# A hybrid state-space and attention network on one core: the seed of the norms' inverse square root moved from VectorE to ScalarE

## The chip, the cores and the metric

The kernel runs on one core of a Trainium2 chip. A core has TensorE (matrix products, PE in the profile), VectorE (DVE), ScalarE (ACT), GpSimd (POOL) and SyncE (SP, which here only issues DMA transfers). The engines have queues of their own, each in program order, and wait for each other through semaphores. The metric is device time in microseconds of one execution; less is better.

## The reference, cut to what matters

The network has four layers on an input of 4 images, 96 channels, 64 x 64 pixels. The first is a state-space layer with two blocks, each of which begins with a norm over the 96 channels of every pixel:

```python
mu = seq.mean(-1, keepdims=True)
var = ((seq - mu) ** 2).mean(-1, keepdims=True)
h = (seq - mu) * jax.lax.rsqrt(var + EPS) * ln_g + ln_b
xz = h @ in_w
...
dA = jnp.exp(delta[..., None] * A)
dBx = delta[..., None] * Bm[:, :, None, :] * xc[..., None]
hstates = jax.lax.associative_scan(comb, (dA, dBx), axis=1)[1]
y = jnp.einsum('blds,bls->bld', hstates, Cm) + Dp * xc
```

The recurrence runs over the 4096 pixels of an image, for 192 channels with 16 states each. A sparse quadratic layer and two attention layers with feed-forward parts follow; the change does not touch them.

## The kernel before

`_mamba` computes the first layer, `_back` the rest; the state-space stage takes the first 3120 us or so of the span. In it the pixels are cut into 8 chunks of 512. A **unit** is one chunk of one pair of images in one of the two blocks: 32 units. A unit has 24 **steps** (three groups of channels, four rows, two halves): 768 steps. `steps` lists them, and one loop over them emits the instructions of all engines in an order written out by hand (`tc.manual_schedule()`), so that each engine's program order is fixed when the kernel is built.

What a step s does, by the names of the code:

- `copies`: SP brings the step's decays in a DMA of 512 KB with a broadcast (tile `a`, six buffers, L434), five steps ahead; now and then also `db`.
- `broadcasts`: TensorE spreads the step's inputs over the 128 partitions into PSUM (tile `pq`, three buffers, L447), two steps ahead. `pq` of step s+2 reuses the buffer of step s-1, so it waits for that step's scans.
- `decays`: ScalarE takes the exponential (L452).
- `product`: VectorE multiplies `pq` by the broadcast B (L457). In the steps that `apart` picks, four of a unit, GpSimd does it on `db` instead.
- `scans`: VectorE runs two scans of 512 (tile `hs`, L470), and between them the next step's product. GpSimd multiplies the states by C (tile `hc`, L476). `hs` and `hc` hold two steps each, in two buffers: a scan two groups later needs that `hc` has read the old `hs`.
- `states` (ScalarE, L480) keeps the last state, `reduce` (TensorE, `py`, L488, every second step) sums over the states, into four groups of 32 partitions, `gate` (VectorE L496, GpSimd L497, every eighth step) finishes y.

Beside the steps there is side work of the units to come: generators `norm`, `front`, `tail` and `rest`, of which the class `Side` advances one in a slot of each step. A generator hands its slot on with a `yield "gap"`. `front` makes the next unit's inputs; among its GpSimd work are `du` (L339) and `ul` (L355), each three per unit. `rest` puts two bn_stats (L408) on VectorE in the units of the first image pair or the second, every other unit or so.

`norm` makes the normalized input of the unit after next. TensorE subtracts the mean (`mm_xc`), ScalarE squares, TensorE forms the variances `mm_v` of 2 images x 512 pixels as a tile of 128 x 8, and ScalarE adds epsilon (`ve`, L221). Then the inverse square root is made by Newton's method from a guess that comes from the bits of the float: half of the bit pattern, taken from a constant. VectorE does that guess (L223, L224) and half of the negative variance (`vh`, L225); GpSimd does three Newton steps in twelve small instructions (L227 to L230). ScalarE copies three columns of history in the same slot (`hn`, L234). TensorE spreads the result over the channels (`mm_r`, L240), one image at a time since PSUM has one buffer for `mm`, and VectorE multiplies (`hn`, L249), once for each image.

Of the kernel before, what the change touches and what calls it, by code (L numbers as in the profile page):

```python
# [9 lines left out]
F32 = mybir.dt.float32  # L10
F32R = mybir.dt.float32r
I32 = mybir.dt.int32
# [3 lines left out]
AF = mybir.ActivationFunctionType  # L16
ALU = mybir.AluOpType
# [25 lines left out]
def _load(nc, pool, src, shape, name, dtype=F32):  # L43
    t = pool.tile(shape, dtype, name=name, tag=name)
    nc.sync.dma_start(t, src)
    return t


def _mamba(ctx, tc, io, w, fd, fstats, xsums):
# [9 lines left out]
    nc = tc.nc  # L59
    wp = ctx.enter_context(tc.tile_pool(name="mw", bufs=1))  # L60
# [30 lines left out]
    red = _load(nc, wp, io["k_red"].rearrange("c (j m) -> c j m", j=4), [128, 4, 32], "red")  # L91
    ctr = _load(nc, wp, io["k_center"], [C, C], "ctr")
    low = _load(nc, wp, io["k_low"], [128, 2], "low")
    mean1 = wp.tile([C, 1], F32, name="mean1", tag="mean1")
    nc.gpsimd.memset(mean1, 1.0 / C)

# [73 lines left out]
    def tag(unit):  # L170
        return "_".join(map(str, unit))

    def mm(nm, unit, shape=None):
        return ps_mm.tile(shape or [128, TC], F32, name=f"mm_{nm}{tag(unit)}", tag="mm")

    def tl(nm, unit, shape, dtype=F32, bufs=1, to=None):
        return work.tile(shape, dtype, name=f"{nm}_{tag(unit)}", tag=to or nm, bufs=bufs)
# [9 lines left out]
    def norm(unit):  # L187

        ch, l, pr = unit
        bs = (2 * pr, 2 * pr + 1)  # L190
        xc, sqs, ps = {}, {}, {}

        def centred(n):
            xc[n] = tl(f"xc{n}", unit, [C, TC])
            nc.scalar.copy(xc[n], ps[n])
            sqs[n] = tl(f"sq{n}", unit, [C, TC])
            nc.scalar.activation(sqs[n], xc[n], AF.Square)

        for n, b in enumerate(bs):
            ps[n] = mm(f"xc{n}", unit, [C, TC])  # L200
            nc.tensor.matmul(ps[n], ctr, seq[b, ch, l], start=True, stop=True)
            if l == 0:
                nc.scalar.activation(
                    tl("xs", unit, [C, TC], to=f"sq{n}"), seq[b, ch, 0], AF.Identity, accum_out=xsums[:, b, ch : ch + 1]
                )
            yield
            centred(n)
            yield "free" if n == 0 else "gap"
        p_v = mm("v", unit, [128, 8])
        for n in range(2):  # L210
            for j in range(4):
                nc.tensor.matmul(
                    p_v[:, n * 4 + j : n * 4 + j + 1], sqs[n][:, j * 128 : (j + 1) * 128], mean1, start=True, stop=True
                )
        yield
        ve = tl("ve", unit, [128, 8])
        it = tl("it", unit, [128, 8], I32)
        r = tl("r", unit, [128, 8])
        vh = tl("vh", unit, [128, 8])
        a = tl("ra", unit, [128, 8])  # L220
        nc.scalar.activation(ve, p_v, AF.Identity, bias=w["eps"])  # L221
        yield "gap"
        nc.vector.tensor_single_scalar(it, ve.bitcast(I32), 1, op=ALU.logical_shift_right)  # L223
        nc.vector.tensor_scalar(r.bitcast(I32), it, -1.0, float(0x5F3759DF), ALU.mult, ALU.add)  # L224
        nc.vector.tensor_scalar(vh, ve, -0.5, None, ALU.mult)  # L225
        for _ in range(3):
            nc.gpsimd.tensor_tensor(a, r, r, ALU.mult)  # L227
            nc.gpsimd.tensor_tensor(a, a, vh, ALU.mult)
            nc.gpsimd.tensor_scalar(a, a, 1.5, None, ALU.add)
            nc.gpsimd.tensor_tensor(r, r, a, ALU.mult)  # L230
        if ch:
            for b in bs:
                hn = hn_buf[b, l]
                nc.scalar.copy(hn[:, 0:3], hn[:, TC:])  # L234
        yield "gap"
        yield "gap"
        for n, b in enumerate(bs):
            p = mm(f"r{n}", unit, [C, TC])
            for j in range(4):
                nc.tensor.matmul(  # L240
                    p[:, j * 128 : (j + 1) * 128],
                    r[:, n * 4 + j : n * 4 + j + 1].to_broadcast([128, C]),
                    ident,
                    start=True,
                    stop=True,
                )
            yield
            yield
            nc.vector.tensor_tensor(hn_buf[b, l][:C, 3:], p, xc[n], ALU.mult)  # L249
            yield "free"  # L250
# [283 lines left out]
    with tc.manual_schedule():  # L534
        for n in (0, 1):
            load(units[n])
        side.front = [weights(0), norm(units[0]), front(units[0])]
        side.drain()
        for s in range(5):
# [7 lines left out]
        for s in range(n_steps + NS):  # L547
# [5 lines left out]
            if at == 0:  # L553
                if n + 1 < len(units) and n + 1 not in late:
                    side.front += ([norm(units[n + 1])] if n == 0 else []) + [front(units[n + 1])]
                    side.norm += [weights(1)] * (n == 0)
            if at == 22 and n + 1 == len(units):
                side.tail.append(way_out(units[n]))
            if at == 3 and 0 < n < len(units):
                if n + 1 in late:  # L560
                    side.front = [tail(units[n - 1]), norm(units[n + 1]), front(units[n + 1])]
                else:
                    side.tail.append(tail(units[n - 1]))
# [5 lines left out]
            if s + 2 < n_steps:  # L569
                unit, k, r, h = steps[s + 2]  # L570
# [16 lines left out]
            if live and s + 5 < n_steps:  # L587
                unit, k, r, h = steps[s + 5]
# [807 lines left out]
@with_exitstack  # L1396
def kernel(ctx: ExitStack, tc: tile.TileContext, io, out):
    nc = tc.nc
    cp = ctx.enter_context(tc.tile_pool(name="common", bufs=1))
    dp = ctx.enter_context(tc.tile_pool(name="scratch", bufs=1, space=DRAM))  # L1400
    w = _shared(nc, cp, io)
    p2 = [[dp.tile([2 * C, TC], F32, name=f"p2_{b}_{n}", tag=f"p2_{b}_{n}") for n in range(NCH)] for b in range(B)]
    fd = [dp.tile([C, L], F32, name=f"fd_{b}", tag=f"fd_{b}") for b in range(B)]
    with tc.tile_pool(name="stats", bufs=1) as fp:
        fstats = fp.tile([C, B, NCH, 6], F32, name="fstats", tag="fstats")
        xsums = fp.tile([C, B, NCH], F32, name="xsums", tag="xsums")
        with ExitStack() as c:
            _mamba(c, tc, io, w, fd, fstats, xsums)
        with ExitStack() as c:
            _back(c, tc, io, w, fd, fstats, xsums, p2, out)  # L1410
# [143 lines left out]
```

## Time and profile before

| | us |
|---|---|
| median of 3 runs | 5290.37 (5288.55 to 5313.22) |
| profiled execution | 5277.23 |
| its span, first to last instruction | 5275.4 |
| busy: VectorE | 4432.0 (84% of the span) |
| busy: TensorE | 4055.2 (77%) |
| busy: GpSimd | 2988.1 (57%) |
| busy: ScalarE | 2695.1 (51%) |

The page divides the span into 40 slices of 132 us and gives the busy share of each in tenths. A row of the groups has the line of the code, the engine, the operation, out<-in with shapes, then the busy time, the mean of one instruction in ns, and the idle time of the engine just before, with what ended it. A row of a timeline has the start in us, the duration, the engine, the line, and in brackets the idle time before it and its releaser. "L470" is line 470 of the code of the kernel before.

### The profile page before, as it was taken

Reading aid. Unit: us, or ns where it says so; the run is one execution under the profiler, and the core shown is the slowest. Engines: PE = TensorE matmul, PEld = TensorE weight load, DVE = VectorE, ACT = ScalarE, POOL = GpSimd, SP = SyncE. Lnnn points to the kernel's source line nnn. Section 1 sums busy time; section 2 is a strip of 40 time slices with the busy share of each in tenths; the row PEclk is TensorE's granted clock in tenths of the full one; section 3 lists DMA queues with packets and bytes.
Section 4 is the critical chain, followed back from the end, with each engine's and each line's share of the span. In section 5 each row is a group of like instructions: output and inputs, shape, how many; then the busy total and the mean of one; then the engine's idle time right before and its main releaser. Section 6 shows DMA issues by size and latency. Waiting matters only on the chain.

```text
span 5275.4 us, 52716 instructions
## 1 busy us (share of the span) xinstructions
PE 4055.2 (77%) x15440; PEld 1763.8 (33%) x15440; DVE 4432.0 (84%) x5735; ACT 2695.1 (51%) x5085; POOL 2988.1 (57%) x2104
## 2 busy tenths in 40 slices
PE   4676767777777777777777636899898889989776
PEld 2122222222222222222222102345454555545565
DVE  2879999999999999999999777878787978787655
ACT  3465656656565565656656420023453545444566
POOL 2778888888888888888888761002130312112122
PEclk7677767677786777767777658999999999999976
DMA  4778878788888878788788674553324233322110
GB/s 99 171 171 197 198 187 203 194 196 201 197 192 195 200 190 194 189 195 202 184 201 202 148 192 139 171 170 100 99 85 145 90 102 94 98 90 76 57 33 21
DMA packets 314045, 800.18 MB, mean 152 GB/s; under 512 B 52247, under 2 KB 58106, under 8 KB 312702
## 3 DMA queue, kind: packets, MB, share of 16 engines
q1 hardware_dynamic: 310174, 790.53, 59.2%
q10 hardware_dynamic: 3584, 6.29, 0.4%
q8 instruction: 123, 2.02, 0.2%
q14 instruction: 164, 1.34, 0.1%
HBM read 703.83 MB, written 67.63 MB: 146 GB/s over the span
## 4 chain that ended last, share of the span: by engine, by line
PE 26%; DVE 26%; issue 17%; ACT 11%; POOL 8%; DMA 5%; SPq 1%; DVEq 0%; POOLq 0%; ACTq 0%
DVE hs L470 12%; PE py L895 10%; DVE pq L457 6%; ACT a L452 3%; DMA a<-ddl 3%; POOL hc L476 3%; PE mm_i L264 2%; DVE z L880 2%; DVE a L1110 2%; PE px L1177 2%; PE ph L1092 2%; PE pa L1078 2%; PE py L488 1%; POOL t L1248 1%; POOL o L1246 1%
## 5 line engine op out<-in xcount | busy, mean ns | idle before, releaser
L476 POOL TENSOR_TENSOR hc<-hs,bc 128x1024 f32<-128x1024 f32 x767 | 1804.8, 2360 | 365.8 <-DVE hs L470 350.0
L470 DVE TENSOR_TENSOR_SCAN hs<-a,hst,pq 128x512 f32<-128x512 f32 x1280 | 1571.9, 1261 | 28.9 <-ACT hst L480 12.8
L895 PE MATMUL py<-z,wk 128*96 128x512 f32 x2304 | 1113.5, 613 | 25.8 <-issue 14.3
L452 ACT ACTIVATE a<-a,aneg 128x512 f32<-128x512 f32 x1280 | 849.4, 712 | 309.5 <-DMA a<-ddl 307.4
L880 DVE TENSOR_TENSOR z<-cp,cp 128x512 f32<-128x512 f32 x1152 | 792.5, 714 | 183.9 <-PE py L895 169.3
L457 DVE TENSOR_TENSOR pq<-pq,bc 128x1024 f32<-128x1024 f32 x640 | 772.9, 1208 | 156.9 <-PE pq L447 156.9
L488 PE MATMUL py<-hc,red 128*32 128x512 f32 x3072 | 609.0, 865 | 14.3 <-POOL hc L476 14.3
L895 PEld LDWEIGHTS py<-z,wk 128*96 128x96 f32 x2304 | 366.5, 169 | 447.7 <-issue 315.6
L447 PE MATMUL pq<-uy,sel 64*128 64x512 f32 x768 | 253.4, 654 | 257.1 <-DVE hs L470 204.7
L1145 POOL MEMSET zz<- 96x2 f32 x16 | 1.6, 98 | 740.8 <-ACT zz L1154 739.4
L264 PE MATMUL mm_i<-hn,wk 97*128 97x512 f32 x512 | 348.7, 817 | 92.5 <-ACT xcv L275 59.7
L1246 POOL TENSOR_TENSOR o<-o,fb 128x384 f16<-128x384 f16 x64 | 70.1, 1096 | 549.4 <-ACT o L1251 549.4
L470 DVE TENSOR_TENSOR_SCAN hs<-pq,hst,db 128x512 f32<-128x512 f32 x256 | 324.8, 1269 | 58.1 <-issue 36.1
L452 ACT ACTIVATE pq<-a,aneg 128x512 f32<-128x512 f32 x256 | 177.1, 692 | 366.6 <-DVE hs L470 336.4
L457 POOL TENSOR_TENSOR db<-db,bc 128x1024 f32<-128x1024 f32 x128 | 301.8, 2358 | 21.8 <-DMA db<-ddu 20.3
L447 PE MATMUL pq<-ux,sel 64*128 64x512 f32 x512 | 166.4, 637 | 186.1 <-DVE hs L470 171.8
L447 PEld LDWEIGHTS pq<-uy,sel 64*128 64x128 f32 x768 | 93.8, 238 | 550.8 <-DVE hs L470 372.1
L264 PEld LDWEIGHTS mm_i<-hn,wk 97*128 97x128 f32 x512 | 117.2, 254 | 297.3 <-issue 204.2
L1177 PE MATMUL px<-bd,a 128*96 128x128 f32 x1024 | 148.6, 294 | 67.5 <-DVE a L1110 57.1
L1146 POOL TENSOR_TENSOR zz<-zz 96x256 f32<-96x256 f32 x128 | 122.3, 955 | 135.5 <-ACT zz L1153 83.4
L447 PEld LDWEIGHTS pq<-ux,sel 64*128 64x128 f32 x512 | 61.4, 232 | 384.7 <-DVE hs L470 275.4
L275 ACT ACTIVATE xcv<-mm_i,pvec 128x512 f32<-128x512 f32 x96 | 65.8, 685 | 213.8 <-PE mm_i L264 108.8
(286 smaller groups left out, 6645.8 us busy)
## 6 DMA issues: line engine op xcount, KB each, us to landing
a<-ddl SPq DMA_DIRECT2D x768, 512.0 KB, 7.3
cp<-p SPq DMA_DIRECT2D x480, 192.0 KB, 2.7
db<-ddu SPq DMA_DIRECT2D x128, 512.0 KB, 7.6
bc<-ddb SPq DMA_DIRECT2D x64, 512.0 KB, 8.4
cp<-p SPq DMA_DIRECT2D x480, 64.0 KB, 2.6
ddl<-dl SPq DMA_DIRECT2D x128, 192.0 KB, 3.5
tw_k_fwd<-in_k_fwd SPq DMA_DIRECT2D x64, 256.0 KB, 3.6
tw_k_inv<-in_k_inv SPq DMA_DIRECT2D x64, 256.0 KB, 3.0
```

The costliest lines, as they stand in the source:

```text
L264: nc.tensor.matmul(p, wt[:, 0:128], hn_buf[bs[k], l][:, cols], **f)
L447: nc.tensor.matmul(pqs[s][:, i, :], sel[rows, r, :], made[unit][6][k][h][rows], start=True, stop=True)
L452: nc.scalar.activation(to[:, i, :], das[s][:, i, :], AF.Exp, scale=acol(s, i))
L457: engine.tensor_tensor(t, t, bc(unit, 2, k, h), ALU.mult)
L470: nc.vector.tensor_tensor_scan(hss[g][:, at, :], d0[:, i, :], d1[:, i, :], hst[pr, l, g % 12][:, at : at + 1], ALU.mult, ALU.add)
L476: (nc.gpsimd if s + 1 < n_steps else nc.vector).tensor_tensor(hcs[g][:, sl, :], hss[g][:, sl, :], bc(unit, 3, k, h), ALU.mult)
L488: nc.tensor.matmul(pys[unit, k][32 * (i // 2 + i % 2 * 2) :][:32], red[:, r, :], hc[:, i, :], start=(r == 0), stop=(r == 3))
L880: nc.vector.tensor_tensor(zs[n], cps[q, r0], cps[q, r1], ALU.mult)
L895: nc.tensor.matmul(pys[q], wk[k // KG][:, k % KG, :], zs.pop(n), start=(k == 0), stop=(k == NE - 1))
L1146: nc.gpsimd.tensor_tensor(z0[:, :, 0, :], z0[:, :, 0, :], z1[:, :, 0, :], ALU.add)
L1177: nc.tensor.matmul(p[:, j, :], a2[i % 2][:, kk, :], tabs["bd"][:, int(kk > 0), :], start=True, stop=True)
L1246: nc.gpsimd.tensor_tensor(o2.rearrange("p j c -> p (j c)"), os.pop(g), d["fb2"], ALU.add)
```

## The change

The guess and the half of the negative variance are made on ScalarE. The bit pattern is read as an integer, multiplied by -0.5 and added to the constant, which comes as a bias from a new tile `magic`; the result is written as an integer. `vh` follows directly on `ve`; `r` comes after the generator's "gap", where VectorE's three instructions stood. The tile `it` falls away. GpSimd's Newton steps are the same, and now wait for ScalarE. In the new kernel's program ScalarE has 64 instructions more, VectorE 96 fewer, GpSimd one memset more; the order of all the others is the same on every engine, and the number of ScalarE's table loads too.

```diff
@@ _mamba
+    magic = wp.tile([128, 1], F32, name="magic", tag="magic")
+    nc.gpsimd.memset(magic, float(0x5F3759DF))
@@ norm
         ve = tl("ve", unit, [128, 8])
-        it = tl("it", unit, [128, 8], I32)
         r = tl("r", unit, [128, 8])
         vh = tl("vh", unit, [128, 8])
         a = tl("ra", unit, [128, 8])
         nc.scalar.activation(ve, p_v, AF.Identity, bias=w["eps"])
+        nc.scalar.activation(vh, ve, AF.Copy, scale=-0.5)
         yield "gap"
-        nc.vector.tensor_single_scalar(it, ve.bitcast(I32), 1, op=ALU.logical_shift_right)
-        nc.vector.tensor_scalar(r.bitcast(I32), it, -1.0, float(0x5F3759DF), ALU.mult, ALU.add)
-        nc.vector.tensor_scalar(vh, ve, -0.5, None, ALU.mult)
+        nc.scalar.activation(r.bitcast(I32), ve.bitcast(I32), AF.Identity, bias=magic, scale=-0.5)
         for _ in range(3):
             nc.gpsimd.tensor_tensor(a, r, r, ALU.mult)
```

## The prediction

> **What bounds the kernel now.** I read the page first (busy times and slices), then the groups by form in the state-space stage, then the timelines of VectorE, GpSimd and TensorE around one of the edited places.
>
> ```profile
> DVE  2879999999999999999999777878787978787655
> POOL 2778888888888888888888761002130312112122
> ```
>
> The change lies in the first 3120 us. There VectorE is busy nine tenths or more in most slices and GpSimd eight. The window from 395 to 2810 us, which holds 26 equal units of 92.9 us, gives VectorE 2271.9 of 2415 us (94%), GpSimd 2085.5 (86%), ScalarE 1467.9 (61%), the DMA engines 82%. So VectorE seems to set the pace, with GpSimd close behind.
>
> ```profile
> L224 DVE TENSOR_SCALAR r<-it 128x8 int32<-128x8 int32 x32 | 62.3, 1946 | 1.1
> L225 DVE TENSOR_SCALAR vh<-ve 128x8 f32<-128x8 f32 x32 | 33.8, 1056 | 0.0
> L223 DVE TENSOR_SCALAR it<-ve 128x8 int32<-128x8 int32 x32 | 24.8, 775 | 32.2 <-ACT ve L221 32.2
> ```
>
> These three are what the change takes away. Eight elements per partition should not take 1 to 2 us, and their shortest cases are 165, 172 and 159 ns. The medians are 903, 2275 and 1305 ns. The timeline of VectorE says where the rest goes:
>
> ```profile
> 1505.47 0.72 DVE L496 SCALAR_TENSOR_TENSOR y<-xcv,pvec,py 128x512 f32<-128x512 f32 x1
> 1506.11 0.91 DVE L223 TENSOR_SCALAR it<-ve 128x8 int32<-128x8 int32 x1
> 1507.05 2.27 DVE L224 TENSOR_SCALAR r<-it 128x8 int32<-128x8 int32 x1
> 1509.23 1.31 DVE L225 TENSOR_SCALAR vh<-ve 128x8 f32<-128x8 f32 x1
> 1510.46 1.27 DVE L470 TENSOR_TENSOR_SCAN hs<-a,hst,pq 128x512 f32<-128x512 f32 x1
> ```
>
> and that of GpSimd what it was doing meanwhile, and afterwards:
>
> ```profile
> 1504.47 2.51 POOL L339 TENSOR_TENSOR du<-dl,xcv 128x512 f32<-128x512 f32 x2
> 1506.94 2.35 POOL L476 TENSOR_TENSOR hc<-hs,bc 128x1024 f32<-128x1024 f32 x1
> 1509.25 1.27 POOL L497 TENSOR_TENSOR y<-y,zs 128x512 f32<-128x512 f32 x1
> 1510.47 1.27 POOL L339 TENSOR_TENSOR du<-dl,xcv 128x512 f32<-128x512 f32 x1
> 1511.70 0.20 POOL L227 TENSOR_TENSOR ra<-r 128x8 f32<-128x8 f32 x1
> ...
> 1515.06 2.35 POOL L476 TENSOR_TENSOR hc<-hs,bc 128x1024 f32<-128x1024 f32 x1
> 1517.37 1.28 POOL L355 TENSOR_TENSOR ul<-du,ux 128x512 fp32r<-128x512 f32 x1
> 1518.59 2.37 POOL L476 TENSOR_TENSOR hc<-hs,bc 128x1024 f32<-128x1024 f32 x1
> 1520.91 1.29 POOL L355 TENSOR_TENSOR ul<-du,ux 128x512 fp32r<-128x512 f32 x1
> 1522.13 4.86 POOL L476 TENSOR_TENSOR hc<-hs,bc 128x1024 f32<-128x1024 f32 x2
> ```
>
> The reader is to see two things. Each of the three ends as one GpSimd instruction ends (1506.94, 1509.25, 1510.47): VectorE stands still for 4.35 us. And GpSimd has no gap from 1502.15 to 1528.2: in just this part of the unit it is the fuller engine.
>
> [...] half of the four reductions takes as long as all four. The trace agrees: 1.93 us for x8 (at 1518.28), and where GpSimd came late:
>
> ```profile
> 3026.35 1.92 PE L488 MATMUL py<-hc,red 128*32 128x512 f32 x4 [4.05 <-POOL hc L476]
> ```
>
> **The change part by part.** *VectorE loses 96 instructions.* Start to next start, the three take 4.35 us in 23 of the 27 units from 394 to 2814 us, 3.20 to 4.26 in four: 115 us in all. In the five other units GpSimd is idle and they take 0.36 us.
>
> *How much of a unit's 4.35 us survives.* VectorE's order is otherwise the same in the built program, and so is GpSimd's. I replay the unit above with VectorE 4.35 us earlier. GpSimd's chain does not move: du, hc, y, du and the Newton steps (L227 to L230, 1511.70 to 1515.06) were never waiting for VectorE's three. The third hc after Newton still ends at 1524.5. Behind it, in TensorE's order, stand the reduction py (L488), then mm_r (L240) for the second image, and only then can VectorE do its second hn (L249), with the next scan queued behind. Earliest second hn = 1524.5 + 0.1 (semaphore) + py half (1.0 at the fast clock, 1.86 at the slow one; both occur) + mm_r to hn (2.06 wherever VectorE waited for it) = +3.2 to +4.0, I take +3.66. Today it starts at 1528.45, +3.95. So this unit keeps 0.3 us of 4.35; VectorE waits at hn instead. (A smaller stop on the way: the scan of the group after next needs hc's buffer read, 1517.4 against 1516.6.)
>
> Every second unit also has two bn_stats (L408) on VectorE there; in these the second hn starts +5.45 after the third hc on average, counted without GpSimd's own 0.19 us wait. They keep 1.8 us. Sum of the differences: 14 units without (mean 4.05) x 0.39 = 5.5, 13 with x 1.79 = 23.3: **29 us**. All at the slow clock (4.0) it is 20 us; with mm_r at the fast clock too (2.25) 67.
>
> *Starved units.* VectorE waits for ve in order in three units: 3.95 us at 111, 7.45 at 235, 15.36 at 2951. The scan behind it had its inputs (at 2951: exp done 2936.65, db 2935.03). Freed, VectorE does that step in the gap, and the broadcast pq on TensorE, which waited 3.9 us for it ahead of mm_r, no longer does. Newton's end (2955.39) then gates mm_r: first hn at 2957.4 instead of 2959.94, 2.5 us, and the same in the other two. **7 us**; at least 0 if these shifts meet a later wait, at most 15 (half of the 26.8 us waited, rounded up).
>
> *ScalarE gains 64 instructions.* Nearest row: ve, 267 ns, start to next start 0.17. No conversion from int32 on ScalarE is in the trace; a cast to fp32r of 512 columns takes 0.60 against 0.56 for a copy, so between 0.17 and 0.54 us each, I take 0.2. At most 35 us over a stage in which ScalarE idles 39%; the next exp waits 1.75 us for its DMA. Taken at nothing. No table load is added: 129 in both built orders.
>
> *The new wait:* Newton on GpSimd waits for r from ScalarE. In the built order r stands just before the copies hn (L234), which start at 1507.37, Newton at 1511.70; the smallest such margin in the 27 units is 3.5 us. Behind Newton on GpSimd stand the hc, and behind these VectorE's scans. Nothing, while the margin holds.
>
> *GpSimd gains one memset* (about 0.1 us, among the opening ones while loads are under way): nothing. The queue of SP issues the same; its copies a wait for VectorE's scans, 1242 us in all, and move earlier with these, except where they stand behind ux and uy, which wait for GpSimd's ul. With 82% of the DMA engines' time used, 40 us less in 3000 adds 1%: nothing.
>
> Sum: 29 + 7 = **36 us**. The profiled execution took 5277.2 us (span 5275.4 and 1.8 around it), 13 us under the median of the runs, 5290.4. Taken from the median: **5254 us**, 0.7% less. A measurement of this kernel can tell about 0.5%, 26 us, from no change.
>
> **The rivals.**
>
> *Full recovery.* VectorE's share of 94% says that it bounds, and 115 us come back, with the starved units' part about 125: 5165 us. For it: VectorE waits only 96 us for pq and 7 for mm_r from 395 to 2900 us. Against it: GpSimd's unbroken 26 us in each unit. Chance 0.12.
>
> *Nothing to measure.* TensorE stays at the slow clock behind the wait, units without bn_stats keep nothing, starved units give it back: 10 to 20 us, 5275. For it: most mm_r there took 2.06 us, the slow form. Chance 0.24.
>
> *Slower.* ScalarE reaches r late: the exp ahead of it waits for DMA a (12.3 us the longest, 285 in all). From 3.5 to 4.3 us of lateness on, each us delays Newton, hc, py and hn one to one, in the chain that now sets the pace. At 2 us beyond the margin in all 27 units it is +54: 5344. Against it: r's place was reached 3.5 us early in every unit. Chance 0.05.
>
> *It doesn't do what it says:* the built order shows it does; no chance given.
>
> The main case has 0.59.
>
> **How the numbers follow.** The main case runs from 20 + 0 to 67 + 15 us of gain: 5208 to 5270. The range 5185 to 5288 takes in most of the second rival and the lower part of a partial recovery, leaving out the full one and the slow one. Faster by over 0.5% (under 5264): 0.12 and 0.54 of the main case: 0.66. Within 0.5%: 0.24 and the other 0.05: 0.29. Slower: 0.05.
>
> **What would show it.** Right: L223 to L225 gone from VectorE, its busy time 121 us less, and of that most found again as waits of hn (L249) for mm_r, now 26 us, then about 110; GpSimd's hc waiting less than 329 us for scans; unit length about 91.8 us instead of 92.9. Wrong: if hn waits little and the unit shrinks to 88.6 us, VectorE was the bound after all; if GpSimd waits for r from ScalarE, the slow rival; if the three starved places keep their gap on VectorE, that step.

## The result, and the profile after

| | before | after |
|---|---|---|
| median of 12 runs each, us | 5287.37 | 5293.53 |
| ratio after / before, 95% interval | | 1.0013 [0.9996, 1.003] |
| profiled execution's span, us | 5275.4 | 5291.6 |
| VectorE busy, us | 4432.0 | 4322.7 |

The change makes no difference that can be measured. The forecast was 36 us less, and the interval excludes it: it reaches from 2 us less to 16 us more. VectorE was nevertheless relieved, by 109 us of busy time. The page of the kernel after, first VectorE's and GpSimd's slices, then the share of each engine in the chain that ended last:

```profile
DVE  2888898888988889888898877888787878787655
POOL 3778888888888888888898861002130322112122
...
PE 29%; DVE 19%; issue 14%; ACT 11%; POOL 10%; DMA 9%; SPq 2%; DVEq 0%; POOLq 0%; ACTq 0%
```

The share of each engine in the chain before the change:

```profile
PE 26%; DVE 26%; issue 17%; ACT 11%; POOL 8%; DMA 5%; SPq 1%; DVEq 0%; POOLq 0%; ACTq 0%
```

The row of nines of VectorE has become mostly eights; GpSimd's row is nearly what it was. In the chain VectorE fell from 26 to 19%, and DMA rose from 5 to 9%. From 395 to 2900 us alone, the DMA of `a` rose from 6.2 to 14.3% of the chain. The groups by form (busy time, mean ns of one, idle time before and what ended it) show the moved instructions and their neighbours:

```profile
L249 DVE TENSOR_TENSOR hn<-mm_r,xc 96x512 f32<-96x512 f32 x64 | 43.7, 683 | 76.4 <-PE mm_r L240 75.5
L227 POOL TENSOR_TENSOR ra<-r 128x8 f32<-128x8 f32 x96 | 19.3, 201 | 38.1 <-ACT r L225 15.9 <-ACT hst L480 11.7 <-ACT hn L234 5.5
L225 ACT ACTIVATE r<-ve,magic 128x8 int32<-128x8 int32 x32 | 9.5, 296 | 0.0
L223 ACT ACTIVATE vh<-ve 128x8 f32<-128x8 f32 x32 | 6.7, 209 | 1.0
```

So 16 us of busy time on ScalarE do what took VectorE 121. Of VectorE's three instructions before the change, each of the 79 cases that took over 0.4 us ended 0.03 us after the end of a GpSimd instruction; why is not shown. GpSimd's Newton steps waited for ScalarE in five units, 33.1 us in all (the row names `r` or a neighbour of it on ScalarE), in the same five in which they had waited 39.6 us for VectorE's `vh`. The wait of `hn` for `mm_r` grew from 26 to 76 us, where about 110 were forecast.

Where did the time go? The waits from 395 to 2900 us (engine and line, what it waited for: total us, times, longest) say it. ScalarE and VectorE after:

```profile
ACT a L452 <- DMA a<-ddl: 334.5, 183, 5.1
ACT pq L452 <- DMA a<-ddl: 231.4, 29, 9.4
...
DVE pq L457 <- PE pq L447: 171.6, 80, 4.7
DVE hn L249 <- PE mm_r L240: 44.0, 40, 2.4
```

and both before, in the same window:

```profile
ACT pq L452 <- DVE hs L470: 292.5, 81, 7.4
ACT a L452 <- DMA a<-ddl: 228.6, 144, 3.6
...
DVE pq L457 <- PE pq L447: 96.0, 66, 4.4
DVE hn L249 <- PE mm_r L240: 7.1, 14, 0.7
```

Before, the largest wait of the exponentials was for VectorE's scans, and that for the decays `a` came second, 229 us. After, they wait for the DMA of `a` in both forms, 566 us. VectorE's product waits 172 us for `pq` where it waited 96. The wait of SP for GpSimd's `ul`, which stands ahead of some of these DMAs in SP's queue, grew too. Before, then after:

```profile
SPq L345 <- POOL ul L355: 161.7, 54, 4.6
```

```profile
SPq L345 <- POOL ul L355: 249.4, 54, 8.4
```

The chain of waits of the kernel after, in order of time (start, us, what), passes through this place:

```profile
1448.17 5.62 DMA a<-ddl
...
1454.45 0.71 ACT a L452
1455.15 0.58 ACT xcv L275
1455.78 3.78 PE mm_i L264 x4
...
1526.85 1.24 POOL ul L355
...
1528.10 0.57 SPq L345
...
1531.99 7.79 DMA a<-ddl
```

It runs from GpSimd's `ul` to SP's copies of ux and uy, to the `a` behind them, 7.79 us on its way, and from an `a` over the exponential to the copy `xcv` that stands behind it on ScalarE, to TensorE's `mm_i`. VectorE's `hn`, the place at which the forecast let the saved time end, is not on it.

The same unit as in the prediction, in SP's timelines (the DMA issues). Before, VectorE's second `hn` starts at 1528.45:

```profile
1528.24 0.52 SPq L345 DMA_DIRECT2D ux<-ul  x1
...
1531.76 1.21 SPq L434 DMA_DIRECT2D a<-ddl  x2
```

and after:

```profile
1537.48 0.52 SPq L345 DMA_DIRECT2D ux<-ul  x1
...
1541.03 1.21 SPq L434 DMA_DIRECT2D a<-ddl  x2
```

VectorE's timeline after has the second `hn` of this unit, with the wait for `mm_r` ahead of it in brackets:

```profile
1536.12 0.69 DVE L249 TENSOR_TENSOR hn<-mm_r,xc 96x512 f32<-96x512 f32 x1 [1.23 <-PE mm_r L240]
```

`hn` comes earlier within GpSimd's work, but ux, uy and the `a` behind them do not: the pair of `a` starts 3.3 us after `hn` before and 4.9 us after it now. In the mean of the 23 units of the table below, the first `a` behind these copies is issued 2.7 us after `hn` before and 5.3 us now.

Cutting each unit at four events gives the balance. The table holds means over the units 5 to 27, in us, taken from the starts in the traces (even and odd units averaged apart, then together; one profiled execution of each kernel). The events are the second `hn`, ScalarE's first and second copy `xcv` (L275), the last instruction of Newton on GpSimd, and the next unit's second `hn`. The lower rows belong to the experiments. A unit's length is set by a few discrete waits, so a mean of one execution is uncertain by up to some 0.5 us in the sum, and 0.3 in the second and third stretch (estimated from the scatter of the units).

| kernel | hn to 1st xcv | to 2nd xcv | to Newton's last | to next hn | sum |
|---|---|---|---|---|---|
| before | 10.81 | 8.16 | 59.81 | 14.39 | 93.2 |
| after | 12.17 | 9.25 | 60.64 | 12.02 | 94.1 |
| a_stall | 11.03 | 8.20 | 59.85 | 14.15 | 93.2 |
| a_noseed | 12.15 | 9.15 | 60.68 | 12.07 | 94.0 |
| a_copies_first | 10.74 | 8.91 | 60.84 | 12.75 | 93.2 |
| a_deep7 | 10.74 | 9.16 | 60.52 | 11.78 | 92.2 |
| b_deep7 | 10.72 | 8.21 | 59.76 | 14.14 | 92.8 |
| a_reduce_later | 13.78 | 8.88 | 60.52 | 10.48 | 93.7 |
| a_deep7_reduce_later | 11.56 | 8.95 | 61.13 | 10.49 | 92.1 |
| a_newton1 | 11.57 | 8.58 | 57.76 | 12.75 | 90.7 |
| b_newton1 | 10.73 | 7.75 | 57.21 | 16.60 | 92.3 |
| a_deep7_newton1 | 10.74 | 8.74 | 58.24 | 12.79 | 90.5 |
| b_deep7_newton1 | 10.73 | 8.11 | 57.42 | 16.49 | 92.7 |

From before to after the last stretch shrinks by 2.4 us: this is what was saved. The first three grow by 1.4, 1.1 and 0.8: this is where it went. The difference of 0.9 us for each of the 23 units, 20 us, is about the 16 us by which the profiled span is longer; over many runs only some 6 us of it are left.

### The profile page after: what moved, and what is told of

Its sections match the earlier page's. It is cut to its first block, busy times and chain, and to the rows that moved or that the text cites. A ratio compares the mean times of both kernels' runs of the same rounds, so it can differ in the third digit from the quotient of the medians.

```text
span 5291.6 us, 52686 instructions
## 1 busy us (share of the span) xinstructions
PE 4093.0 (77%) x15440; PEld 1748.6 (33%) x15440; DVE 4322.7 (82%) x5639; ACT 2706.8 (51%) x5149; POOL 2990.1 (57%) x2105
## 3 DMA queue, kind: packets, MB, share of 16 engines
q8 instruction: 123, 2.02, 0.2%
## 4 chain that ended last, share of the span: by engine, by line
PE 29%; DVE 19%; issue 14%; ACT 11%; POOL 10%; DMA 9%; SPq 2%; DVEq 0%; POOLq 0%; ACTq 0%
PE py L895 10%; DVE hs L470 8%; DMA a<-ddl 7%; POOL hc L476 4%; DVE pq L457 4%; PE mm_i L264 3%; ACT a L452 3%; DVE z L880 2%; PE py L488 2%; PE px L1177 2%; DVE a L1110 2%; PE mm_i L267 2%; PE ph L1092 2%; PE pa L1078 2%; POOL du L339 1%
## 5 line engine op out<-in xcount | busy, mean ns | idle before, releaser
L488 PE MATMUL py<-hc,red 128*32 128x512 f32 x3072 | 671.2, 841 | 50.4 <-POOL hc L476 50.1
L264 PE MATMUL mm_i<-hn,wk 97*128 97x512 f32 x512 | 325.1, 768 | 152.5 <-ACT xcv L275 127.4
L275 ACT ACTIVATE xcv<-mm_i,pvec 128x512 f32<-128x512 f32 x96 | 65.5, 682 | 214.6 <-PE mm_i L264 123.4
L1177 PEld LDWEIGHTS px<-bd,a 128*96 128x96 f32 x1024 | 130.7, 176 | 113.2 <-DVE a L1110 70.4
```

Source lines behind the costliest of these rows:

```text
L264: nc.tensor.matmul(p, wt[:, 0:128], hn_buf[bs[k], l][:, cols], **f)
L488: nc.tensor.matmul(pys[unit, k][32 * (i // 2 + i % 2 * 2) :][:32], red[:, r, :], hc[:, i, :], start=(r == 0), stop=(r == 3))
L1177: nc.tensor.matmul(p[:, j, :], a2[i % 2][:, kk, :], tabs["bd"][:, int(kk > 0), :], start=True, stop=True)
```

## The experiments

The expectations speak of **theory A**: VectorE's stop was not what set the pace, because beside it there ran a chain of nearly the same length, GpSimd's unbroken work and, behind it, the copies of `a` that come late (called A1; A2 is a variant that blames TensorE's order, in which the reduction `py` stands ahead of the side work). The rivals are the cost of ScalarE's new instructions, and, where an expectation says so, other bounds. Ratios are to the kernel before on the same chip. Its own medians there lie between 5280 and 5288 us, so a difference in us between two experiments can be off by several us.

### One Newton step, with and without the change

```diff
-        for _ in range(3):
+        for _ in range(1):
```

a_newton1 makes this edit in the changed kernel, b_newton1 in the kernel before.

> The changed kernel with one Newton step on GpSimd instead of three (two of the three refinements of the inverse square root are left out, 8 of 12 small instructions, 2.25 us of GpSimd's time per unit). Theory A, GpSimd's unbroken stretch (du, hc, y, Newton, hc, ul) and what hangs on it in SP's queue set the pace of a unit: 29 units x 2.25 us, about 60 us less than the changed kernel's 5293, so 5235. Theory B, the pace is set by ScalarE, to which the change gave 0.5 us per unit: no difference, 5290. Theory C, VectorE is still the bound: no difference either.

> The kernel before with one Newton step instead of three (the same part is left out). Theory A says that before the change VectorE with its 4.35 us of standing still and GpSimd's stretch ran side by side and were about equally long; then a shorter stretch alone gives less than in the changed kernel: 0 to 25 us, 5262 to 5287. If the two kernels gain the same 60 us, GpSimd's stretch alone bounded before the change, too, and VectorE's three instructions never mattered.

Measured: a_newton1 5221.4 us, ratio 0.9856 [0.982, 0.9893], 72 us under the changed kernel. b_newton1 5253.7, 0.9934 [0.9903, 0.9964], 34 us under the kernel before, more than the 0 to 25 that were expected. Shortening GpSimd's work by about 2.3 us pays in both, twice as much where VectorE has no stop. The table shows why: in b_newton1 Newton ends 2.6 us earlier and the next `hn` takes 2.2 us longer from there (16.60 for 14.39). VectorE's own queue, with the stop in it, then sets `hn`. So before, it seems, two chains of nearly equal length met at `hn`.

a_newton1 shows the late `a` too. In its even units the first `xcv` comes 12.2 us after `hn` and a unit takes 93.9 us; in its odd units, 10.9 and 87.4. (Even and odd units differ in other work too: before, they took 94.5 and 91.8 us.)

### VectorE's stop put back, its result unused

```diff
+        it, r2, vh2 = tl("it", unit, [128, 8], I32), tl("r2", unit, [128, 8]), tl("vh2", unit, [128, 8])
+        nc.vector.tensor_single_scalar(it, ve.bitcast(I32), 1, op=ALU.logical_shift_right)
+        nc.vector.tensor_scalar(r2.bitcast(I32), it, -1.0, float(0x5F3759DF), ALU.mult, ALU.add)
+        nc.vector.tensor_scalar(vh2, ve, -0.5, None, ALU.mult)
         nc.scalar.activation(r.bitcast(I32), ve.bitcast(I32), AF.Identity, bias=magic, scale=-0.5)
```

> The changed kernel with VectorE's three instructions put back where they stood, now on tiles that nobody reads; the seed still comes from ScalarE. VectorE has its old order and stands still 4.35 us per unit again; ScalarE's 64 instructions and GpSimd's new wait remain. Theory A, the stop was hidden beside GpSimd's stretch and what follows it: as the changed kernel, 5285 to 5300. Theory B, the change did win on VectorE and lost as much on ScalarE: 30 us or more above the changed kernel, 5320 to 5400, since now both costs are paid.

Measured: 5282.7 us, ratio 1.0005 [0.9989, 1.0021]: the same as the kernel before and as the changed one. Its groups by form have VectorE's stop back:

```profile
L228 DVE TENSOR_SCALAR r<-it 128x8 int32<-128x8 int32 x32 | 62.4, 1949 | 1.1
```

and its ScalarE waits as it did before, not as after:

```profile
ACT pq L456 <- DVE hs L474: 284.6, 81, 7.4
ACT a L456 <- DMA a<-ddl: 225.7, 152, 3.6
```

The stop alone switches between the two pictures, row for row in the table (11.03 and 14.15 against 12.17 and 12.02), and the time stays. So in this kernel, with all else as it is, 105 us of busy time more or less on VectorE are free, and the late `a` is a result of their absence and not of ScalarE's new instructions, which a_stall keeps.

### No seed at all

a_noseed leaves out the guess on both engines; Newton starts from 1, with three steps of the same instructions. `magic` now holds minus half of epsilon.

```diff
-        nc.scalar.activation(ve, p_v, AF.Identity, bias=w["eps"])
-        nc.scalar.activation(vh, ve, AF.Copy, scale=-0.5)
+        nc.scalar.activation(ve, p_v, AF.Identity, bias=magic, scale=-0.5)
         yield "gap"
-        nc.scalar.activation(r.bitcast(I32), ve.bitcast(I32), AF.Identity, bias=magic, scale=-0.5)
...
+            seed = r if n else one
```

> The changed kernel with no seed at all: Newton starts from the constant 1 (left out: the guess from the bits, so that the inverse square root is less exact), and ScalarE makes minus half of the variance directly in its one old instruction. Neither VectorE's three nor ScalarE's two are in it. Theory A: as the changed kernel less at most ScalarE's 0.5 us in 29 units, 5278 to 5293. Theory B, ScalarE's two instructions took the gain: the 36 us of the prediction or more come back, under 5257.

Measured: 5301.5 us, ratio 1.0038 [1.0021, 1.0055], a little above what was expected and not below the changed kernel. Its picture is that of after:

```profile
ACT a L452 <- DMA a<-ddl: 351.7, 195, 4.7
ACT pq L452 <- DMA a<-ddl: 231.2, 28, 9.5
```

With ScalarE's 64 instructions gone, `a` is as late and the unit as long (94.0 us). They took nothing away.

### TensorE's order

a_reduce_later emits the reduction after the slot of side work, so that `mm_r` need not stand behind it; a_deep7_reduce_later does so with the seventh buffer of the next section.

```diff
-            if s % 2 == 1 and 2 < s <= n_steps + 1:
-                reduce(s // 2 - 1)
             side.slot()
             if n == 0 or n + 1 in late:
                 side.slot()
+            if s % 2 == 1 and 2 < s <= n_steps + 1:
+                reduce(s // 2 - 1)
```

> The changed kernel with reduce (py) emitted behind the slot of its step, so that on TensorE mm_r no longer stands behind a py that waits for GpSimd's hc. Nothing is left out. Theory A2, the wait of hn for mm_r takes the gain: that wait falls from 44 us to under 15, time 5250 to 5265. Theory A1, SP's queue and the a behind it set the pace: the wait at hn falls but the time found goes to the wait for pq, 5280 to 5300.

> The changed kernel with the seventh buffer for a and reduce behind the slot. Nothing is left out. If the late a and the wait at hn are the two things that took the gain, both together give more than the buffer's 43 us: 5205 to 5230. If side work on TensorE and ScalarE (mm_i, xcv, the two table loads, mm_o) is a third chain of the same length, no more than the buffer alone: 5240 to 5255.

Measured: 5309.1 us, ratio 1.0054 [1.0036, 1.0073], slower than the kernel before and than the changed one; with the buffer 5252.8, 0.9934 [0.9911, 0.9956], no better than the buffer alone. The wait of `hn` nearly goes, from 44 to 2.8 us from 395 to 2900 us, and others take its place: VectorE's `y` waits 79 us for the reduction, and GpSimd's `hc` waits for it to free its buffer:

```profile
POOL hc L476 <- PE py L488: 240.7, 87, 5.6
```

The wait for `pq`, to which A1 gave the time, did not grow (148 us after 172). Since the edit brings waits of its own, the two times alone do not refute A2, and the second of them is also what a third chain on TensorE and ScalarE would give. The table says more. In a_reduce_later `hn` comes 1.5 us sooner after Newton's end than in the changed kernel (10.48 for 12.02), but the first `xcv` does not: from Newton's end to it there are 24.3 us in one and 24.2 in the other. So `hn` is not what sets the `xcv` there; a wait that vanishes is no gain where it was not the last to end.

### A seventh buffer for `a`

a_deep7 (the changed kernel) and b_deep7 (the kernel before) bring `a` six steps ahead instead of five. The room comes from two tiles that now lie in columns of `dl`.

```diff
-        das[s] = scan.tile([128, 2, TC], F32, name=f"a_{name(s)}", tag="a", bufs=6)
+        das[s] = scan.tile([128, 2, TC], F32, name=f"a_{name(s)}", tag="a", bufs=7)
...
-            if live and s + 5 < n_steps:
+            if live and s + 6 < n_steps:
...
-                copies(s + 5)
+                copies(s + 6)
```

> The changed kernel with seven buffers for a instead of six, and the copies six steps ahead instead of five; room is made by putting dbl and dh into columns of dl. Nothing is left out. Theory A1, what holds the changed kernel up is that the copies of a stand in SP's queue behind ux and uy, which wait for GpSimd's ul, and ScalarE's exponentials then wait for a with xcv, and TensorE's mm_i and pq, behind them: ScalarE's wait for DMA a falls from 566 us (395 to 2900 us) to under half, VectorE's wait for pq from 172 to 100 or less, time 5220 to 5245. Theory A2, TensorE's order (py, mm_r, hn) alone takes the gain: 5285 to 5293, the wait of hn for mm_r unchanged.

> The kernel before with the same seventh buffer. Theory A1: VectorE with its 4.35 us bounds there, so little comes of it: 5270 to 5287. If it gains as much as the changed kernel does, the late copies cost both kernels the same, and the buffer says nothing of where the change's gain went.

Measured: a_deep7 5250.7 us, ratio 0.9918 [0.9885, 0.9951], 43 us under the changed kernel; b_deep7 5273.7, 0.9971 [0.9952, 0.9991], 14 us under the kernel before. The direction of A1 is confirmed: b_deep7 lies in the range expected, a_deep7 6 us above it. One sign did not come: VectorE's wait for `pq` fell from 172 to 144 us only, where 100 or less were expected. The wait of `hn` for `mm_r` stays (38 us after 44). ScalarE's waits in a_deep7:

```profile
ACT pq L450 <- DVE hs L468: 308.9, 82, 8.7
...
ACT a L450 <- DMA a<-ddl: 102.6, 70, 3.5
```

The wait of the form `pq` for the DMA is gone, that of the form `a` is under a third, and the first `xcv` is back at 10.74 us after `hn`. The second stretch of the unit stays long (9.16), so the buffer returns a part only. b_deep7 is the control: there ScalarE's wait for `a` falls from 229 us to 2.4, and the kernel gains only 14 us. Before the change the late `a` was mostly not the last to end.

### The order of SP's queue alone

a_copies_first keeps six buffers and five steps, and issues the copies of `a` ahead of the slot in which ux and uy are issued.

```diff
+            ahead = False
+            if live and s + 5 < n_steps:
+                unit, k, r, h = steps[s + 5]
+                if unit in made and not (apart(s + 5) and len(made[unit][5]) <= k):
+                    copies(s + 5)
+                    ahead = True
             side.slot()
...
-            if live and s + 5 < n_steps:
+            if live and s + 5 < n_steps and not ahead:
```

> The changed kernel, in which the copies of a and db for five steps ahead are issued before the side work of the step instead of after it and the scan; the number of buffers stays. On SP's queue they then stand ahead of that step's ux and uy copies, which wait for GpSimd's ul. Theory A (what is given back comes from SP's order: the copies of a stand behind ux and uy): the exponentials wait for a clearly less, under 220 us in the groups of a from 395 to 2900 us where the changed kernel had 335, and the time comes to 5250 to 5275 us. Theory B (the copies wait for a buffer that a scan has yet to free, the order does not matter): waits as in the changed kernel, 5285 to 5300 us.

Measured: 5280.0 us, ratio 0.999 [0.9972, 1.0009]: between the two expectations, 14 us under the changed kernel. The interval overlaps that of the changed kernel, so the time alone settles nothing. The waits and the table say more. The first `xcv` is at 10.74 us, as early as with the seventh buffer, so it is the order in SP's queue that had delayed it. Half of the 1.4 us won there is lost again ahead of the next `hn` (12.75 us for 12.02), and the unit is 0.8 us shorter. And ScalarE still waits for `a`, 262 us where under 220 were expected:

```profile
ACT pq L452 <- DVE hs L470: 292.8, 81, 8.5
ACT a L452 <- DMA a<-ddl: 262.1, 89, 7.3
```

because the copies, now ahead of ux and uy, wait longer in the queue for the scans that free their buffers (1169 us against 960). Order and depth both count.

### Both relieved, with and without the change

a_deep7_newton1 and b_deep7_newton1 put the seventh buffer and the single Newton step together: the two chains beside VectorE's are both shorter.

> The changed kernel with seven buffers for a, copies six steps ahead, and one Newton step for three (left out: two refinements of the inverse root). Theory A (GpSimd's stretch and the late a are what keep VectorE's saved time from showing; with both relieved the kernel is free to take it): the two gains add, 72 and 43 us below the changed kernel, so 5165 to 5200 us. Theory C (a third chain, TensorE's side work from the first xcv to pq at the slow clock, already holds the unit near 91 us): no lower than with one Newton step alone, 5210 to 5240 us.

> The kernel before with the same two edits: VectorE still makes the seed and stands still for it. Theory A: its 4.35 us per unit are now on the path, so it stays 40 to 70 us above the changed kernel with these edits, 5225 to 5255 us. Theory C: the same third chain holds both, so the two are within 20 us of each other.

Measured: a_deep7_newton1 5198.7 us, ratio 0.9826 [0.98, 0.9852]; b_deep7_newton1 5271.2, 0.9975 [0.9955, 0.9995]. So the seed's place is worth 72 us here, between two kernels that differ in nothing else. The medians of all four pairs, in us:

| beside it | seed on VectorE | seed on ScalarE | gain |
|---|---|---|---|
| nothing | 5287.4 | 5293.5 | -6 |
| seventh buffer | 5273.7 | 5250.7 | 23 |
| one Newton step | 5253.7 | 5221.4 | 32 |
| both | 5271.2 | 5198.7 | 72 |

In the first pair the interval of the ratio includes no change; in each of the others the intervals of the two ratios do not overlap, though in the second they only just do not. In the table of stretches the gain of the last pair lies in the last stretch, 12.79 us against 16.49; the second and third together are 1.45 us longer. In a_deep7_newton1 VectorE has no stop of its own there, and its wait of `hn` for `mm_r` has come down to 19.5 us as well (VectorE's waits, 395 to 2900 us):

```profile
DVE pq L455 <- PE pq L445: 124.9, 72, 4.1
...
DVE hn L249 <- PE mm_r L240: 19.5, 27, 1.4
```

Theory C, by which a third chain would hold both kernels at the same length, falls. a_deep7_newton1 has the lowest median of all these kernels, 86 us below the one before (its interval overlaps that of a_newton1). The gain on the changed kernel, 95 us, is less than the two single gains together (115), but its time lies in the range that theory A gave. b_deep7_newton1 was expected at 5225 to 5255 us and came out higher; that it is no faster than b_newton1 (5253.7 us; the intervals just overlap) was not expected and stays open.

## Why the prediction failed, point by point

**What bounds.** "GpSimd has no gap" was right: from `du` to the last Newton step GpSimd's stretch took 10.43 us before and 10.47 after, so it did not move. That most of VectorE's 4.35 us would be swallowed there was not: 2.4 of them arrived at `hn`.

**The surviving part (29 us).** Up to `hn` the gain was there, and larger than forecast: 2.4 us per unit against a mean of 1.1 (14 units at 0.39 and 13 at 1.79). The way from the end of the third `hc` to the second `hn`, put at 3.66 us, measured 2.46 in the mean of the 23 units (4.64 before). Its term for `mm_r` was too large: from `mm_r` to `hn` 2.06 us were taken, and it took 1.15 in 20 of the 23. The group `mm_r` ran in 1.11 us there, which it had done in 3 of the 23 units before. This is near the upper case of the forecast, 67 us. The forecast's fast and slow clock stand in both traces as a granted clock of 1.00 and 0.50: in these units `mm_r` took 1.11 us at the one and 2.02 at the other, the four reductions 1.06 and 1.93 in the median, half of them 1.05 and 1.92. A reduction that waited for `hc` began 0.05 us after its end, where 0.1 was taken. Why TensorE was granted the faster clock at `mm_r` more often than before stays open.

**The step that failed** is the sentence that the copies of SP "move earlier with these, except where they stand behind ux and uy, which wait for GpSimd's ul", priced at "nothing". The exception is just what decides. `hn` moved forward against GpSimd, `ul` hardly: the third `ul` ended 0.6 us ahead of `hn` before and ends 1.1 us behind it now. So ux, uy and the `a` behind them come later as seen from `hn`, the exponential waits, and with it the `xcv` behind it on ScalarE. That takes 1.4 us of the 2.4; a_copies_first, which changes only SP's order, has the `xcv` back where it was. The sum was made up to `hn`, with the rest of the unit taken as unchanged. But `hn` is only one of two ways from Newton into the next unit; the other goes over `ul` and SP's queue. For each of the two the time has to be worked out. From Newton's end to the first `xcv` it was 25.2 us before (14.39 + 10.81) and 24.2 after: that is the 1.0 us per unit that really came free at this point.

**The remaining 1.9 us** (1.1 up to the second `xcv`, 0.8 up to Newton's end) are only partly explained. Between the two `xcv` TensorE does a group of four `mm_i` that takes from 1.98 to 3.78 us. It took over 3 us in 20 of the 23 units after (mean 3.6 us), and in 15 before (mean 3.1 us): half of the 1.1. In the traces of all 13 kernels (299 such units) it took over 3.3 us in each of the 81 in which TensorE had stood idle for 4 us or more ahead of it, and under 3 us in 50 of the 95 with less than 2 us of idle time. That idle time was 1.2 to 3.6 us before and is 3.4 to 6.1 us after. In the traces before and after, the group took 1.98 us where the granted clock was 1.00 and 3.73 to 3.78 where it was 0.50 to 0.51; its mean over the groups fell from 0.68 to 0.53. After the change it was 0.50 to 0.51 in all 17 units with 4 us or more of idle time; before, in the 16 units with less than 2 us, it was 1.00 in eight and 0.50 to 0.54 in eight. No run here holds the clock fixed, so that the idle time brings the lower clock is argued and not shown. a_deep7, in which the first `xcv` is on time, keeps it: the idle time there is 3.4 us, and the group took over 3.1 us in every unit. The other half, and the 0.8 us up to Newton's end, stay open.

**Starved units (7 us).** Not settled. The first two of the three places were to give 2.5 us each; the unit after them starts at 320.4 instead of 325.5 us, which fits. But a_noseed, in which VectorE has no stop either, starts it at 326.3, so one execution does not show it. At the third, GpSimd's wait fell from 12.3 to 4.6 us; that unit is 17 us shorter than before in the profiled execution, but b_newton1, with the seed on VectorE, has it as short (100.7 us), so nothing follows from that.

**ScalarE's 64 instructions (nothing).** Right: a_noseed. The 0.2 us taken for one was close: 0.21 for `vh`, 0.30 for `r`.

**The new wait (nothing).** Right: GpSimd waited for ScalarE only in the five units, the first four and the last, in which it had waited for VectorE before, 33 us in all after 40. The slow rival's mechanism did not occur.

**The rivals.** The time came nearest to that of "Nothing to measure" (5275 us), by another cause: its reason was that TensorE stays slow behind the wait (the granted clock was 1.00 at `mm_r` in 20 of the 23 units) and units keep nothing up to `hn`, and they kept more than forecast. Full recovery is refuted by the measured time, and by a_stall. Three of the signs named came out otherwise: the waits of `hn` reached 76 us and not 110, GpSimd's `hc` waited longer for scans (348 us after 329, from 0 to 2990 us), and the unit grew to 94.1 us instead of shrinking to 91.8.

## What to carry to other kernels

An engine that stands still for 4 us in every round can be cut free of it without a gain (5293.5 us after for 5287.4 here), when a second chain of the same length bypasses the place: before pricing a relief, follow every path from the last common event into the next round, those over the DMA queues too, and take the longest. In SP's queue here the `a` behind ux and uy waited for what these wait for, GpSimd's `ul` (249 us from 395 to 2900 us after the change); since `ul` hardly moved, `a` did not either, however early its consumer was ready. Test such a claim cheaply by putting the removed work back on unread tiles, and relieve the chains together before calling any one of them worthless: the same edit was worth nothing alone, 23 or 32 us beside one relief, and 72 us beside both.

## What the runs showed of the hardware that was not expected

- **Integer input and output cost ScalarE little here.** `r` with int32 on both sides took 296 ns for 128 x 8, `ve` with float on both sides (read from PSUM) 261, `vh` with an immediate scale and no bias tile 209.
- **What SP's issuing queue waited for mattered more here than the time its issues took.** A transfer of `a` took 7.6 us in the median after the change, and an issue 0.5 to 0.6. SP's 1410 issues from 395 to 2900 us took 768 us together, its waits more: 960 us for scans and 249 us for `ul` alone. The seventh buffer, which moves the copies in that queue a step ahead, gave 43 us in the changed kernel.
